# Last unit of an expert layer: its rows reach their tokens by products with one-hot matrices, in place of scatters and reloads

## The chip, the cores and the metric

The kernel runs on one core of one Trainium2 chip. The metric is the device time of one execution in microseconds (us), the median over runs. The core has five engines that work side by side, each in the order of its own instructions: TensorE (PE), VectorE (DVE), ScalarE (ACT), GpSimd (POOL) and SyncE (SP), which here only issues DMAs. POOL also issues the indirect DMAs (gathers and scatters).

## The reference, cut to what matters

The input is x, 16 batches of 1024 tokens of 256 floats. The output is x + attention(xn) + experts(xn), with xn the layer norm of x. The part around the change is the expert layer:

```python
scores = jnp.einsum('ntd,de->nte', x, gate_w)
probs = jnp.transpose(jax.nn.softmax(scores, axis=-1), (0, 2, 1))
g, m = jax.lax.top_k(probs, k)                  # k = 256 tokens for each batch and expert
xin = jax.vmap(lambda xb, mb: xb[mb])(x, m)
h = jax.nn.gelu(jnp.einsum('nekd,edf->nekf', xin, w1))
h = jnp.einsum('nekf,efd->nekd', h, w2)
weighted = g[..., None] * h
out = jnp.zeros((n * t, d)).at[flat_idx].add(weighted.reshape(-1, d))
return out.reshape(n, t, d).astype(jnp.bfloat16)
```

Each of 8 experts picks its 256 tokens of highest probability in each batch, runs them through two layers (256 to 1024, gelu, 1024 to 256), weighs the rows by their probability and adds them to the tokens that they came from. The sum over experts is rounded to bfloat16 and then added to x and attention.

## The kernel before

**Stages.** The attention comes first (some 560 us). It leaves in DRAM, for every batch, `xg` (the normalized rows and gate values), `xa` (x plus attention) and `acc` (zeros, in which the experts' rows are summed). The indices of the chosen tokens lie in `idxT`, on the partitions of the rows that they belong to.

**Units.** The rest is a loop over 64 units. A unit is one expert with one pair of batches: 512 rows, in four quarters q of 128 (q = 2t + k: half t is one batch, k its first or second 128 rows). The batches come in three groups (4, 6 and 6), and inside a group the experts follow one another, each over all pairs. The last three units are expert 7 with the batches 10 and 11, 12 and 13, 14 and 15; instructions of the last two bear 12 and 14 in their tiles' names.

**Order.** The order of every engine's work is written out by hand: what the Python code calls first is issued first. While unit n computes, the rows of unit n+2 are gathered and those of n+1 laid out. `layer1` (L767) has two rounds r = 0, 1, each with three PSUM banks pa, pb, pc of which each gets two products. In each round DVE computes `u2` from pb (L792), later `u3` from pb (L801) and `c22` from pc (L803). PE can begin the second product in pb only when L792 has read it, and the second in pc (after both rounds) only when L803 has. `layer2` (L840) makes the rows y1 (half 1) and y0 (half 0): L899, L903, L904, L905 and L917 on DVE, `fourth_sum` (L836) on POOL, and `weigh` (L867), the multiplication with the probability, on ACT.

**Scatters.** `scatter(y, t, k)` (L871, the DMA at L873) adds the 128 rows of a quarter to their tokens in `acc` of the batch, as an indirect DMA of POOL. The two scatters of a batch write the same tensor, so the second has a wait for the first one's landing. y1's scatters are issued in `layer2`; y0's in `rest`, which runs in the next unit's `layer1`, after the first products of its round 0.

**Finish.** The output is made in 64 parts, four for each batch: a part is two of the eight tokens that each partition holds, 128x512 floats or 256 KB, and token number = 8 x partition + j. A part loads `xa` (`load_x`) and `acc` (`load_a`), adds the bias (`bias`, L994, DVE), rounds acc to bfloat16 (`cast`, L990, ACT), adds (`add`, L999, DVE) and stores (`store`, L1003, SP). `plan` hangs these steps into slots of the units: "first" (ahead of a unit's layer 1), "s1", "s2" (round 0), "s3" (round 1), "middle" (after layer 1), "lay" (in layer 2, where other units lay out the next), "s4" (late in layer 2), and "end" (after the last unit). Lists: `first`, eight parts of batches 11 and 10, done in the last unit; `second` (in the loop `nearly`), batches 13 and 12, reloaded in the last unit's "middle", with their adds after the last unit; `third` (in the loop `last`), batches 15 and 14, reloaded (L986) when the last unit's own scatters have landed.

The tail of `run`, after the last unit:

```python
pending.pop()(lambda: None)          # rest of the last unit: the scatters
for k, p in enumerate(nearly):
    ...
for step in at.pop((NU, "end")):     # five biases
    step()
done.load_last_a()
for p in last:
    done.cast(p)
    done.add(p)
    done.store([p])
```

Of the kernel before, what the change touches and what calls it, by code (L numbers as in the profile page):

```python
# [8 lines left out]
F32 = mybir.dt.float32  # L9
BF16 = mybir.dt.bfloat16  # L10
U32 = mybir.dt.uint32
AF = mybir.ActivationFunctionType
ALU = mybir.AluOpType
AX = mybir.AxisListType

P = 128
# [7 lines left out]
def tile_linear_attn_expert_choice_moe(  # L24
# [648 lines left out]
    with ExitStack() as fctx:  # L673
# [163 lines left out]
                u.half_sum(0, r), u.block(1, 0, r), u.half_sum(1, r), ALU.subtract  # L837
            )

        def layer2(u, rows, w2_sb, wt, lay_out_next, slot, more_sums):  # L840
            (b11, _), (b21, b22) = out_weights(w2_sb)
            t1, t2, t3, t4 = (wt[:, i, :, :] for i in range(4))

            def hidden(i, t):
                return u.hT[:, i * ND : (i + 1) * ND, t * HT : (t + 1) * HT]

            def product(bk, a, b, start=True):
                for k in range(NS):
                    for c in range(ND):
                        nc.tensor.matmul(  # L850
                            bk[:, k * EH : (k + 1) * EH], a[:, c, k * P : (k + 1) * P],
                            b[:, c, :], start=start and k == 0 and c == 0, stop=True,
                            skip_group_check=True,
                        )

            def two(bk):
                return bk[:, 0:E].rearrange("p (k d) -> p k d", k=NS)

            def new(k):
                return bank(f"q{k}{u.e}_{u.b0}")  # L860

            def temp(tag):
                return u.temp(tag, "y")[:, 0, :].rearrange("p (k d) -> p k d", k=NS)

            def weigh(y, t, k, cols, in_):
                q = t * NS + k
                nc.scalar.activation(  # L867
                    y[:, k, cols], in_, AF.Copy, scale=rows[:, q, E + u.e : E + u.e + 1]
                )

            def scatter(y, t, k):  # L871
                b, ix = index(u.e, u.b0, t * NS + k)
                nc.gpsimd.indirect_dma_start(  # L873
                    out=acc[b], out_offset=bass.IndirectOffsetOnAxis(ap=ix, axis=0),
                    in_=y[:, k, :], in_offset=None, compute_op=ALU.add,
                )

            y0, y1 = (
                hpool.tile([P, NS, E], F32, tag="y", name=f"y{t}{u.e}_{u.b0}", bufs=4)
                for t in range(2)  # L880
            )
            px, pw = new("x"), new("w")
            product(px, hidden(0, 0), b11)
            p1 = temp("p1")
            nc.scalar.copy(p1, two(px))
            first_sum(u, 1)
            product(pw, hidden(1, 1), t4)
            for r in range(2):
                second_sum(u, r)
            pz = new("z")  # L890
            product(pz, u.sums[:, 0, :, :], t1)
            for r in range(2):
                third_sum(u, r)
                fourth_sum(u, r)
            lay_out_next()
            py = new("y")
            product(py, u.sums[:, 1, :, :], t2)
            u2 = temp("u2")
            nc.vector.tensor_tensor(u2, two(py), p1, ALU.add)  # L899
            pv = new("v")  # L900
            product(pv, hidden(0, 1), t3)
            u3 = temp("u3")
            nc.vector.tensor_tensor(u3, two(pv), u2, ALU.add)  # L903
            nc.vector.tensor_tensor(y1[:, :, EH:E], two(pz), u3, ALU.add)  # L904
            nc.vector.tensor_tensor(y1[:, :, 0:EH], two(pw), u3, ALU.add)  # L905
            for k in range(NS):
                weigh(y1, 1, k, slice(0, E), y1[:, k, :])
            scatter(y1, 1, 0)
            if more_sums:
                more_sums()  # L910
                scatter(y1, 1, 1)
            product(px, hidden(1, 0), b21, False)
            for k in range(NS):
                weigh(y0, 0, k, slice(0, EH), px[:, k * EH : (k + 1) * EH])
            slot("s4")
            product(pz, u.sums[:, 0, :, :], b22, False)
            nc.vector.tensor_tensor(y0[:, :, EH:E], two(pz), u2, ALU.add)  # L917

            def rest(between):
                for k in range(NS):  # L920
                    weigh(y0, 0, k, slice(EH, E), y0[:, k, EH:E])
                scatter(y0, 0, 0)
                if not more_sums:
                    scatter(y1, 1, 1)
                between()
                scatter(y0, 0, 1)

            return rest


# [4 lines left out]
        class Finish:  # L935
            def __init__(self):
                self.todo = [
                    (b, slice(j, j + 2))
                    for h, e, b0 in units if e == NE - 1
                    for b in (b0 + 1, b0) for j in range(0, NJ, 2)  # L940
                ]
                self.x, self.a, self.s = {}, {}, {}

            def part(self, t, p):
                b, j = self.todo[p]
# [52 lines left out]
            def add(self, p):  # L998
                nc.vector.tensor_tensor(self.x[p], self.x[p], self.s[p], ALU.add)  # L999

            def store(self, ps):
                for p in ps:
                    nc.sync.dma_start(self.part(out, p), self.x[p])  # L1003

        def plan():

            done, at = Finish(), {}

            def put(n, place, step, *args):
                at.setdefault((n, place), []).append(lambda: step(*args))  # L1010

            of = [[p for p, (b, _) in enumerate(done.todo) if b in g] for g in GROUPS]
            ends = [max(n for n, u in enumerate(units) if u[0] == h) + 2 for h in range(3)]

            for k, p in enumerate(of[0] + of[1]):
                n, place = ends[0] + k, "s2"
                if k >= len(of[0]):
                    k -= len(of[0])
                    n = ends[1] + k
                    if n > NU - 7:  # L1020
                        n, place = n - (NU - 6) + ends[1] + 2, "s4"
                put(n - 1, "first", done.load_x, p)
                put(n - 1, "first", done.load_a, p)
                put(n - 1, "s4", done.cast, p)
                put(n, place, done.bias, p)
                put(n, place, done.add, p)
                put(n, place, done.store, [p])

            first, second, third = (of[2][i * 2 * QT : (i + 1) * 2 * QT] for i in range(3))
            assert len(of[2]) == 6 * QT  # L1030
            for k, p in enumerate(first):
                put(NU - 6, "first", done.load_x, p)
                put(NU - 5 + k // 4, "s2" if k % 4 < 2 else "s4", done.bias, p)
                put(NU - 2, "middle", done.load_a, p)
                put(NU - 1, ("s1", "s2", "s3", "lay")[k // 2], done.cast, p)
            put(NU - 3, "first", done.load_last_x)
            for p in second:
                put(NU - 1, "middle", done.load_a, p)
            places = [(NU - 3, "s4")] * 3 + [
                (NU - 2, place) for place in ("s1", "s1", "s2", "s2", "s3", "s4", "s4")  # L1040
            ] + [(NU - 1, "s1")] + [(NU, "end")] * 5
            for p, (n, place) in zip(second + third, places):
                put(n, place, done.bias, p)
            for k, p in enumerate(first):
                place = "s2" if k < 2 else "s3" if k < 4 else "lay"
                put(NU - 1, place, done.add, p)
                put(NU - 1, place, done.store, [p])
            return at, done, second, third

        def run(gen, first):  # L1050
# [19 lines left out]
            def add_sums(n):  # L1070
                for _ in range(n):
                    if sums:
                        sums.pop(0)()
# [10 lines left out]
            for n, (h, e, b0) in enumerate(units):  # L1084
# [14 lines left out]
                def between():  # L1099
                    add_sums(2)  # L1100
                    if n + 2 < NU:
                        rows[n + 2] = gather(*units[n + 2])
# [17 lines left out]
                def lay_out_next():  # L1120
# [4 lines left out]
                    else:  # L1125
# [3 lines left out]
                pending.append(  # L1129
                    layer2(  # L1130
                        u, rows[n], w2s[i], wts[i], lay_out_next, slot,
                        None if final else lambda: add_sums(2),
                    )
                )
                del rows[n]
# [3 lines left out]
            for k, p in enumerate(nearly):  # L1139
                if k >= QT:  # L1140
                    done.cast(p)
                done.add(p)
                done.store([p])
            for step in at.pop((NU, "end")):
                step()
            done.load_last_a()
            for p in last:
                done.cast(p)
                done.add(p)
                done.store([p])  # L1150
            assert not at
# [46 lines left out]
```

## Time and profile before

| what | value |
|---|---|
| median of 3 runs | 2180.11 us (2178.78 to 2180.33) |
| the profiled execution | 2178.58 us |
| its span | 2176.9 us |
| PE busy | 2125.7 us (98%) |
| DVE busy | 1757.8 us (81%) |
| POOL busy | 1357.8 us (62%) |
| ACT busy | 861.9 us (40%) |
| granted clock of TensorE over the span | 0.993 |
| last product of PE ends | 2151.2 us |
| last add of DVE ends | 2172.1 us |

All times count from the start of the span. Lines of the profile name the engine, the line of the kernel, the operation and its tiles as out<-in. "Idle before" is the time for which the engine stood still just ahead of an instruction, with what ended the wait as far as semaphores show it; where the engine that is named had long been done, it was something else, often a DMA. A product of float32 shows up as two passes of PE, so 16 passes are 8 products. SPq stands for the DMA queue of SP.

### The profile page before, as it was taken

Reading aid. Unit: us, or ns where it says so; the run is one execution under the profiler, and the core shown is the slowest. Engines: PE = TensorE matmul, PEld = TensorE weight load, DVE = VectorE, ACT = ScalarE, POOL = GpSimd, SP = SyncE. Lnnn points to the kernel's source line nnn. Section 1 sums busy time; section 2 is a strip of 40 time slices with the busy share of each in tenths; the row PEclk is TensorE's granted clock in tenths of the full one; section 3 lists DMA queues with packets and bytes.
Section 4 is the critical chain, followed back from the end, with each engine's and each line's share of the span. In section 5 each row is a group of like instructions: output and inputs, shape, how many; then the busy total and the mean of one; then the engine's idle time right before and its main releaser. Section 6 shows DMA issues by size and latency. Waiting matters only on the chain.

```text
span 2176.9 us, 37218 instructions
## 1 busy us (share of the span) xinstructions
PE 2125.7 (98%) x13556; PEld 1957.1 (90%) x13556; DVE 1757.8 (81%) x3197; ACT 861.9 (40%) x1598; POOL 1357.8 (62%) x1015
## 2 busy tenths in 40 slices
PE   7999999999999999999999999999999999999995
PEld 6888888888899999999999999899999999999994
DVE  6888888886889989679999998767777788776786
ACT  5645546453233333333333333333334343333334
POOL 4545445354577777777666766676676677667743
PEclk9999999999999999999999999999999999999997
DMA  6444535555455555554555555355546665565567
GB/s 200 137 150 142 194 122 171 164 157 172 113 104 107 104 105 112 111 134 94 132 135 112 129 133 132 69 102 103 116 103 159 168 151 124 131 138 106 118 169 213
DMA packets 333767, 290.61 MB, mean 133 GB/s; under 512 B 163856, under 2 KB 285968, under 8 KB 333584
## 3 DMA queue, kind: packets, MB, share of 16 engines
q1 hardware_dynamic: 283168, 217.55, 35.3%
q0 software_dynamic: 49728, 70.29, 18.2%
q8 instruction: 107, 1.75, 0.3%
q14 instruction: 76, 0.62, 0.1%
q10 hardware_dynamic: 688, 0.40, 0.1%
HBM read 153.36 MB, written 101.19 MB: 117 GB/s over the span
## 4 chain that ended last, share of the span: by engine, by line
PE 93%; DVE 3%; issue 1%; DMA 1%; SPq 1%; ACT 1%; POOL 0%; DVEq 0%; ACTq 0%; POOLq 0%
PE pb L771 14%; PE qz L850 10%; PE qx L850 10%; PE pc L771 10%; PE pa L771 9%; PE pk L318 5%; PE qw L850 5%; PE qv L850 5%; PE qy L850 5%; PE pq L387 5%; PE pg L423 5%; PE po L491 5%; PE xt L305 1%; PE qt L469 1%; SPq L685 1%
## 5 line engine op out<-in xcount | busy, mean ns | idle before, releaser
L873 POOL DMA_INDIRECT acc<-y,idxT x256 | 414.7, 1620 | 350.9 <-ACT y L867 201.1
L237 POOL DMA_INDIRECT rows<-xg,idxT x256 | 263.5, 1029 | 79.4 <-issue 70.5
L867 ACT ACTIVATE y<-y,rows 128x256 f32<-128x256 f32 (+1 forms) x256 | 102.6, 450 | 518.1 <-DVE y L905 516.0
L746 ACT ACTIVATE hT<-hT 128x512 f32<-128x512 f32 x384 | 238.3, 632 | 155.2 <-DVE hT L803 94.6
L771 PE MATMUL pb<-ts,ws 128*128 128x256 f32 x1024 | 263.5, 380 | 4.6 <-DVE ts L721 2.4
L771 PE MATMUL pa<-xT,w 128*128 128x256 f32 x1024 | 263.8, 380 | 1.4 <-issue 1.4
L850 PE MATMUL qx<-w,hT 128*128 128x128 f32 x2048 | 249.4, 275 | 0.0
L850 PEld LDWEIGHTS qx<-w,hT 128*128 128x128 f32 x2048 | 243.9, 192 | 3.3
L836 POOL TENSOR_TENSOR sums<-hT,sums 128x512 f32<-128x512 f32 x128 | 172.7, 1367 | 85.5 <-PE qz L850 84.9
L771 PEld LDWEIGHTS pb<-ts,ws 128*128 128x128 f32 x1024 | 194.1, 190 | 32.6 <-POOL ws L713 2.7
L771 PEld LDWEIGHTS pa<-xT,w 128*128 128x128 f32 x1024 | 190.3, 191 | 25.2 <-issue 1.8
L801 DVE TENSOR_TENSOR u<-pb,p 128x512 f32<-128x512 f32 x128 | 88.4, 691 | 113.2 <-PE pb L771 98.3
L746 ACT ACTIVATE hT<-pa 128x512 f32<-128x512 f32 x128 | 76.5, 597 | 170.0 <-PE pa L771 166.0
L785 ACT COPY p<-pa 128x512 f32<-128x512 f32 x128 | 75.1, 586 | 165.9 <-PE pa L771 161.8
L792 DVE TENSOR_TENSOR u<-pb,p 128x512 f32<-128x512 f32 x128 | 88.5, 691 | 64.0 <-ACT y L867 44.5
L771 PE MATMUL pc<-xT,ws 128*128 128x256 f32 x512 | 134.6, 385 | 0.0
L771 PE MATMUL pc<-ts,ws 128*128 128x256 f32 x512 | 132.3, 381 | 0.0
L771 PE MATMUL pb<-ts,w 128*128 128x256 f32 x512 | 131.4, 379 | 0.0
L850 PE MATMUL qw<-wt,hT 128*128 128x128 f32 x1024 | 124.8, 275 | 0.0
L850 PE MATMUL qz<-wt,sums 128*128 128x128 f32 x1024 | 124.8, 275 | 0.0
L850 PE MATMUL qy<-wt,sums 128*128 128x128 f32 x1024 | 124.8, 275 | 0.0
L850 PE MATMUL qz<-w,sums 128*128 128x128 f32 x1024 | 124.8, 275 | 0.0
(142 smaller groups left out, 4753.1 us busy)
## 6 DMA issues: line engine op xcount, KB each, us to landing
rq<-rows SPq DMA_DIRECT2D x1024, 32.0 KB
w<-in_w_dram SPq DMA_DIRECT2D x96, 256.0 KB
w<-in_w_dram SPq DMA_DIRECT2D x48, 512.0 KB
xg<-xn SPq DMA_DIRECT2D x16, 1056.0 KB
x<-in_x_dram SPq DMA_DIRECT2D x32, 512.0 KB
acc<-zero SPq DMA_DIRECT2D x16, 1024.0 KB
xr<-in_x_dram SPq DMA_DIRECT2D x32, 512.0 KB
xa<-xr SPq DMA_DIRECT2D x28, 512.0 KB
```

The lines of the kernel that those rows point to most:

```text
L237: nc.gpsimd.indirect_dma_start(out=rows[:, q, :], out_offset=None, in_=xg[b], in_offset=bass.IndirectOffsetOnAxis(ap=ix, axis=0),)
L318: nc.tensor.matmul(pk[:, 0:KG], t.xnT[:, d, j * P : (j + 1) * P], wkg_sb[:, d, :], start=(d == 0), stop=(d == NC - 1),)
L387: nc.tensor.matmul(pq[:, k * E : (k + 1) * E], t.xnT[:, d, j * P : (j + 1) * P], wq_sb[:, d, :], start=(d == 0), stop=(d == NC - 1),)
L423: nc.tensor.matmul(t.pg[:, c * E : (c + 1) * E], t.xn[:, j, c * P : (c + 1) * P], t.kk[:, j, 0:E], start=(j == 0), stop=(j == NJ - 1),)
L491: nc.tensor.matmul(po[:, k * E : (k + 1) * E], qT[:, c, j * P : (j + 1) * P], t.mo[:, c, :], start=(c == 0), stop=(c == NC - 1),)
L746: nc.scalar.activation(out, in_, AF.Gelu_apprx_tanh)
L771: nc.tensor.matmul(bk[:, j * HT : (j + 1) * HT], w[:, f * P : (f + 1) * P], x, start=start and j == 0, stop=True, skip_group_check=True,)
L792: nc.vector.tensor_tensor(u2, both(pb), p1, ALU.add)
L836: nc.gpsimd.tensor_tensor(u.half_sum(0, r), u.block(1, 0, r), u.half_sum(1, r), ALU.subtract)
L850: nc.tensor.matmul(bk[:, k * EH : (k + 1) * EH], a[:, c, k * P : (k + 1) * P], b[:, c, :], start=start and k == 0 and c == 0, stop=True, s ...
L867: nc.scalar.activation(y[:, k, cols], in_, AF.Copy, scale=rows[:, q, E + u.e : E + u.e + 1])
L873: nc.gpsimd.indirect_dma_start(out=acc[b], out_offset=bass.IndirectOffsetOnAxis(ap=ix, axis=0), in_=y[:, k, :], in_offset=None, compute_op ...
```

## The change

The last unit (batches 15 and 14) no longer scatters. For each of its four quarters a matrix `hot` is built that has, for slot s (partition) and token, a one where the token is that slot's and zero elsewhere: 1024 columns in float32, in eight blocks (one for each j) of 128. POOL fills the tile with token numbers (`iota`, L1009), DVE copies the quarter's indices to a float column (L1019) and compares the tile with it in place (`is_equal`, L1021). The tiles are old ones: `cur` for quarter 0, `wq_sb` and `wo_sb` (512 columns each) for quarter 1, two buffers of the gathered `rows` for quarters 2 and 3.

A part of batch 15 or 14 is then made by `spread`: for each of its two j, two products of 128x128 by 128x256 (k = 0, 1; the hot block with y) summed in PSUM, so 4 a part and 32 in all, after the unit's last product on PE. DVE adds the part of acc without the last unit's rows, which is now reloaded ahead of the unit (`load_last_a` in slot "first"), and rounds to bfloat16 in the same instruction (L1048). `add` and `store` are as before.

Beside that some steps move: the adds and stores of three of the eight `second` parts, and two of the five biases, go from the end into slot "s4" of the last unit, where DVE does them between L905 and L917.

```diff
-        def layer2(u, rows, w2_sb, wt, lay_out_next, slot, more_sums):
+        def layer2(u, rows, w2_sb, wt, lay_out_next, slot, more_sums, final):
...
-            scatter(y1, 1, 0)
-            if more_sums:
+            if not final:
+                scatter(y1, 1, 0)
                 more_sums()
                 scatter(y1, 1, 1)
...
-                scatter(y0, 0, 0)
-                if not more_sums:
-                    scatter(y1, 1, 1)
-                between()
-                scatter(y0, 0, 1)
+                if not final:
+                    scatter(y0, 0, 0)
+                    between()
+                    scatter(y0, 0, 1)
+
+            u.y = (y0, y1)
...
+            def new_hot(self, q, tiles):
+                n = NJ // len(tiles)
+                parts = [t.rearrange("p (j t) -> p j t", t=P) for t in tiles]
+                for i, t in enumerate(parts):
+                    nc.gpsimd.iota(
+                        t, pattern=[[1, n], [NJ, P]], base=i * n, channel_multiplier=0,
+                        allow_small_or_imprecise_dtypes=True,
+                    )
+                self.hot[q] = [t[:, j, :] for t in parts for j in range(n)]
+                self.hot_parts[q] = parts
+
+            def fill_hot(self, q):
+                h, e, b0 = units[-1]
+                _, ix = index(e, b0, q)
+                nc.vector.tensor_copy(self.slots[:, q : q + 1], ix)
+                for t in self.hot_parts[q]:
+                    nc.vector.tensor_scalar(
+                        t, t, self.slots[:, q : q + 1], None, ALU.is_equal
+                    )
+
+            def new_hots_first(self):
+                self.slots = kpool.tile([P, NQ], F32, tag="slots", name="slots")
+                cur = kpool.tile([P, HALF + 2 * K], F32, tag="cur", name="hot0")
+                self.new_hot(0, [cur])
+                self.new_hot(
+                    1, [t.rearrange("p c e -> p (c e)") for t in (wq_sb, wo_sb)]
+                )
+
+            def new_hots_rest(self):
+                for q in range(2, NQ):
+                    t = gpool.tile([P, NQ, XR], F32, tag="rows", name=f"hot{q}")
+                    self.new_hot(q, [t.rearrange("p q d -> p (q d)")[:, 0 : NJ * P]])
+
+            def spread(self, p, y, t):
+                _, js = self.todo[p]
+                pr = bank(f"pr{p}")
+                for i, j in enumerate(range(js.start, js.stop)):
+                    for k in range(NS):
+                        nc.tensor.matmul(
+                            pr[:, i * E : (i + 1) * E], self.hot[t * NS + k][j], y[:, k, :],
+                            start=(k == 0), stop=(k == NS - 1),
+                        )
+                self.s[p] = hpool.tile([P, 2, E], BF16, tag="fb", name=f"fb{p}", bufs=5)
+                nc.vector.tensor_tensor(
+                    self.s[p], pr.rearrange("p (j d) -> p j d", j=2), self.a[p], ALU.add
+                )
...
             put(NU - 3, "first", done.load_last_x)
+            put(NU - 1, "first", done.load_last_a)
+            put(NU - 1, "first", done.new_hots_first)
+            for q, place in enumerate(("s1", "s2", "s3", "lay")):
+                put(NU - 1, place, done.fill_hot, q)
+            put(NU - 1, "s2", done.new_hots_rest)
             for p in second:
                 put(NU - 1, "middle", done.load_a, p)
+            for p in second[0:3]:
+                put(NU - 1, "s4", done.add, p)
+                put(NU - 1, "s4", done.store, [p])
...
-            ] + [(NU - 1, "s1")] + [(NU, "end")] * 5
+            ] + [(NU - 1, "s1")] + [(NU - 1, "s4")] * 2 + [(NU, "end")] * 3
...
-                        None if final else lambda: add_sums(2),
+                        lambda: add_sums(2), final,
...
-                done.add(p)
-                done.store([p])
+                if k >= 3:
+                    done.add(p)
+                    done.store([p])
             for step in at.pop((NU, "end")):
                 step()
-            done.load_last_a()
-            for p in last:
-                done.cast(p)
+            for k, p in enumerate(last):
+                done.spread(p, u.y[1 - k // QT], 1 - k // QT)
                 done.add(p)
                 done.store([p])
```

More of the change, by code (lines that the diff above doesn't have):

```diff
@@ L942, in __init__ @@
                 self.x, self.a, self.s = {}, {}, {}
+                self.hot, self.hot_parts = {}, {}
             def part(self, t, p):
```

## The prediction

> **What bounds the kernel now.** I read the page first. PE is busy 98% of the span at a granted clock of 0.99, so nearly anything that stops PE costs its full length, and what follows PE's last product is pure addition. The chain of waits (the work that ended last, in order of time: start, length, what) gives that end:
>
> ```profile
> 2149.42 1.80 PE qz L850 x16
> 2151.25 0.44 DVE y L917
> ...
> 2152.38 8.08 DMA acc<-y,idxT x2
> ...
> 2160.85 5.88 DMA fa_rq<-acc
> ...
> 2169.46 2.67 DVE fx_ws L999 x4
> ```
>
> PE ends at 2151.2; then two scatters in a row (8.1 us), the reload of acc (5.9), casts and adds. The last add ends at 2169.46 + 2.67 = 2172.13; the span, 2176.9, ends 4.8 later, when the last store has landed. So 25.7 us stand behind PE, and these the change attacks.
>
> The change also puts new work on POOL and DVE beside the last unit's layer 1. So next I read the timeline there, engine by engine (start, length, engine, line, operation, [idle before it <- what ended it]). POOL, which has the scatters of the unit before the last (rows one to four) and its own step of the last unit (row five):
>
> ```profile
> 2125.31 1.80 POOL L873 DMA_INDIRECT acc<-y,idxT  x1 [3.42 <-ACT y L867]
> 2130.15 1.58 POOL L873 DMA_INDIRECT acc<-y,idxT  x1 [3.03 <-ACT y L867]
> 2132.03 1.54 POOL L873 DMA_INDIRECT acc<-y,idxT  x1 [0.30 <-ACT fb L990]
> 2136.64 1.54 POOL L873 DMA_INDIRECT acc<-y,idxT  x1 [3.07 <-ACT fb L990]
> 2143.86 3.69 POOL L836 TENSOR_TENSOR sums<-hT,sums 128x512 f32<-128x512 f32 x2 [5.67 <-PE qz L850]
> ```
>
> In program order these are y1/0, y1/1, y0/0, y0/1. The two of one batch add into the same acc: the second stands idle 3.0 us and starts 4.84 and 4.61 after the first, though the ACT instruction named had long ended. So POOL is blocked until the first has landed. DVE in the same stretch, which layer 1 needs:
>
> ```profile
> 2128.41 0.69 DVE L792 TENSOR_TENSOR u<-pb,p 128x512 f32<-128x512 f32 x1 [0.78 <-PE pb L771]
> 2130.93 0.69 DVE L801 TENSOR_TENSOR u<-pb,p 128x512 f32<-128x512 f32 x1 [0.63 <-PE pb L771]
> 2132.72 0.69 DVE L792 TENSOR_TENSOR u<-pb,p 128x512 f32<-128x512 f32 x1 [0.31 <-PE pb L771]
> 2135.97 0.69 DVE L803 TENSOR_TENSOR hT<-pc,u 128x512 f32<-128x512 f32 x1
> ```
>
> DVE has only 0.3 to 0.8 us to spare before each. PE writes pb again at 2129.86, 0.76 after the first of these has read it, and pc of round 1 again at 2136.77, 0.1 after the last of them ends at 2136.66. A late DVE stops PE at once.
>
> **Part 1: the matrices, which stand in a queue.** The last unit's "first" slot is issued after y1/0 and y1/1 of the unit before and ahead of y0/0 and y0/1. POOL's order becomes: y1/0, y1/1, iota hot0 (1024 columns), two iotas for hot1 (512 each), y0/0, y0/1, iotas hot2 and hot3 (1024 each), then L836. DVE compares hot0 in slot s1, ahead of the first L792; hot2 in s3, ahead of the second L801 and L803. Both engines work in order, so DVE, and with it PE, waits for POOL, and POOL for scatters to land.
>
> No iota is in the trace. Bounds, with the price of a fill of DVE (a TENSOR_SCALAR whose scalar is a column), come from these groups (busy, mean ns):
>
> ```profile
> L246 POOL MEMSET zero<- 128x512 f32 x1 | 0.5, 522 | 0.0
> L79 POOL TENSOR_SCALAR_AFFINE_SELECT mask<-mask 128x128 f32<-128x128 f32 x1 | 0.3, 347 | 0.0
> L365 POOL TENSOR_TENSOR s<-kk 128x1024 f32<-128x1024 f32 x16 | 37.9, 2371 | 65.4 <-DVE kk L332 65.4
> L332 DVE TENSOR_TENSOR kk<-kk,ke 128x1024 f32<-128x1024 f32 x32 | 39.0, 1219 | 0.0
> L289 DVE TENSOR_SCALAR xn<-x,rstd,nm 128x256 f32<-128x256 f32 x4 | 1.8, 488 | 0.9 <-POOL nm L280 0.9
> ```
>
> Memsets of 128 and 512 columns (0.20, 0.52) give 0.82 ns a column: 0.94 for 1024, the low end. TENSOR_TENSOR gives 2.37 (1.28 for 512), the high end. The affine select also works out a pattern: 0.33 less 0.10 fixed (a memset of one column) over 128 columns is 1.8 ns each, 1.9 for 1024. An iota reads nothing, so I take 1.7 and, for 512, 0.9, nearer to that row than to the memset. A fill: L289 takes 0.41 at least for 256 columns, L125 0.28 for 128: 1.0 ns a column and 0.15 fixed, so 1.2 for 1024 (as L332) and 0.67 for 512; the copies of the indices 0.2 each (L356).
>
> The clock, then:
> - A vector instruction of POOL begins 1.0 after the scatter ahead of it (1977.37 to 1978.45): hot0 2131.15 to 2132.85. DVE fills it until 2134.2; with the bias (0.62) behind it, L792 ends at 2135.5, not 2129.1. PE stands 5.6 us, from 2129.9.
> - hot1 is there at 2134.65 and costs no further wait. y0/0 starts 0.35 later (1981.62 to 1981.97), at 2135.0; y0/1 4.6 after it, at 2139.6; hot2 runs 2140.6 to 2142.3. DVE has by then done all of round 0, the fill of hot1 (1.3) included, by about 2140.5, and waits.
> - Fill until 2143.55, two adds (0.62 each), L801, then L803 0.79 after L801's start, with 0.69 of its own: 2146.3 against 2136.66. PE's pc of round 1 comes **9.6 us later**.
>
> The second stall takes the first one in, so they do not add. After it L836 is no hindrance (hot3's iota ends at 2144.0, L836 is wanted at 2143.86 + 9.6). Hot3's fill (1.4 with its copy) falls into DVE's idle 0.70 before L899 and 1.36 before L903: nothing. The eight reloads of acc are moved to SP ahead of the unit (their tiles are free after the transposes that end at 2119.4): at 0.33 to 0.65 an issue done before y1/0's data move, and the stores queued behind them on SP start only at 2129.7: nothing; if they do slow that scatter, the chain above slips by as much, at most the 1 to 2 us that 2 MB take at the 400 GB/s of the last stretch beyond 2125. With the iota bounds the shift is 7.4 to 11.7.
>
> **Part 2: the tail.** Removed: four scatters, the wait for them, eight reloads, eight casts. Added: 32 products of 128x256 on PE. A pg group (16 passes, 8 such products) takes 3.46, so 0.43 each, 13.8 in all: in before's clock 2151.2 to 2165.1. y1 is weighed by then; y0 (L917, then 0.7 on ACT) by 2153.2, and is used from 2158. Per part of four products (1.73 on PE) DVE adds twice: 0.79 until the dependent one can start, 0.61 until the next, 1.40.
>
> But DVE has other work first. From L905's end (2148.9): three adds and two biases, now in s4, at 0.62 (2152.0); L917 (2152.4); one add; four adds that wait for casts on ACT behind y0's weighing (2156.3); three biases (2158.2). Then 8 x 1.40 = 11.2: **2169.4**. So DVE, not PE, ends the tail; from PE alone it would be 2165.1 + 0.2 + 1.4 = 2166.7. Against 2172.13 this gains 2.7. The stores now come 1.4 apart and not 0.6, so less is queued; of the 4.8 behind the last add I take off 0.2. The tail gains **2.9** (5.6 at best).
>
> **The sum.** +9.6 - 2.9 = +6.7 us. The profiled execution took 2178.58, 1.5 below the median of the runs shown (2180.11): 2185.3 by the one, **2186.8** by the median, which I give. A kernel of this length can be told from no change beyond 0.2%, 4.4 us.
>
> **A rule that speaks against it.** The clock can be seen to fall where PE stops (window, then busy times, PEclk third from the end):
>
> ```profile
> 2153.00:2154.00 1.00, 0.00 (x0) 0.00 (x0) 1.00 (x3) 1.00 (x3) 1.00 (x1) 0.99 0.90 328
> 2154.00:2155.00 1.00, 0.00 (x0) 0.00 (x0) 1.00 (x3) 0.47 (x1) 0.70 (x2) 0.50 1.02 371
> ```
>
> It is halved 2.8 us after PE's last product. A stall of 5.6 would do the same; the products then run at half speed for a while (at the start 32 pk passes took 8.46, later 7.12: 1.3 lost). This loss falls before the second stall, which then is only shorter: nothing in my sum, up to 2.8 if the second stall, 2 to 3.4 long, halves the clock too. [...]
>
> **Rivals.**
> - **The matrices' price is higher**, by iotas slower than any row, or the clock lost in the second stall: each us on 1024 columns costs 3 us of shift (hot0, both halves of hot1, hot2). For: POOL's power on 8 columns takes 1.7 us. Against: no simple form does. +9 to +15: 2189 to 2195.
> - **Cheap matrices, a shorter tail**: iotas at the memset's rate (shift 7.4) and the tail set by PE (5.6): +1.8, 2181.9. For: an iota only writes. Against: DVE's list above.
> - **POOL isn't held**: the iotas run while a scatter is in flight. It decides if hot2 is there by 2135.6, 6.7 sooner than I have it. Then only the fills stay: 3.7 and three copies, 4.3 in layer 1, against 2.35 of DVE's idle: 2.0 late, less 2.9: -0.9, 2179.2; by PE's tail -3.6, 2176.5. For: the releaser named in the rows isn't a scatter. Against: every second scatter of a batch stands the same 3.0 idle.
>
> **Chances.** Forecast (+4.4 to +9) 0.53, higher price 0.22, cheap matrices 0.16, POOL not held 0.09. The last two are mostly within 0.2%; a fifth or so of the cheap case comes out slower after all, a third of the last faster. Faster 0.03, same 0.20, slower 0.77. Range: +1.4 (cheap) to +11.9 (TENSOR_TENSOR's rate, 8.8, and 2.8 of clock): 2181.5 to 2192.
>
> **What would show it.** In the changed profile: the DVE compare of hot0 and of hot2 idle with POOL's iota as releaser; PE idle some 5.6 and 2 to 3.4 us in layer 1 of the last unit; PE's last L850 near 2161; DVE without gaps in the last 11 us while PE is ahead of it. I am wrong if the iotas start before y1/1, or if PE shows no gap.

## The result and the profile after

The changed kernel takes 2182.97 us against 2178.45 us for the kernel before on the same chips (medians of 22 runs each; lowest 2181.91 and 2177.18): ratio **1.0022, 95% interval 1.0016 to 1.0028**, or +4.5 us. The forecast was +6.7, the range +1.4 to +11.9. One of the changed kernel's 22 runs (3764.7 us) and two of e5's below (3776.4 and 5833.8) were in a much slower state and are left out of the ratios. The profiled execution took 2182.9, its span 2181.2.

The last unit's first product (PE's first pa, L771) began at 2126.40 before and 2124.81 after, and between 2124.85 and 2127.32 in the experiments that show no new stall ahead of it: single profiles scatter by up to 2.5 us over the 2100 us that the change does not touch. So stretches are counted from that product.

POOL in the timeline of the changed kernel (start, length, engine, line, operation, [idle before <- what ended it]):

```profile
2123.72 1.80 POOL L873 DMA_INDIRECT acc<-y,idxT  x1 [3.43 <-ACT y L867]
2129.58 1.55 POOL L873 DMA_INDIRECT acc<-y,idxT  x1 [4.05 <-ACT hT L746]
2130.58 1.62 POOL L1009 IOTA hot<- 128x1024 f32 x1
2131.57 1.17 POOL L1009 IOTA wq_sb<- 128x512 f32 x1
2132.09 1.66 POOL L1009 IOTA wo_sb<- 128x512 f32 x1
...
2133.92 1.55 POOL L873 DMA_INDIRECT acc<-y,idxT  x1 [0.17 <-issue]
2138.43 1.54 POOL L873 DMA_INDIRECT acc<-y,idxT  x1 [2.96 <-DMA out_dram<-fx]
2139.42 2.58 POOL L1009 IOTA hot<- 128x1024 f32 x2
```

The order is the predicted one: y1/0, y1/1, the iotas, y0/0, y0/1, the iotas. No iota starts before the second scatter of a batch has been let go, 5.86 and 4.51 after the first. DVE and then PE, in the same view:

```profile
2132.23 1.05 DVE L1021 TENSOR_SCALAR hot<-hot,slots 128x1024 f32<-128x1024 f32 x1 [6.73 <-POOL hot L1009]
...
2133.80 0.68 DVE L792 TENSOR_TENSOR u<-pb,p 128x512 f32<-128x512 f32 x1
...
2141.06 1.49 DVE L1021 TENSOR_SCALAR hot<-hot,slots 128x1024 f32<-128x1024 f32 x1 [0.90 <-POOL hot L1009]
...
2151.35 0.75 DVE L1021 TENSOR_SCALAR hot<-hot,slots 128x1024 f32<-128x1024 f32 x1
```

```profile
2134.53 2.08 PE L771 MATMUL pb<-ts,ws 128*128 128x256 f32 x4 [6.10 <-DVE slots L1019]
...
2145.13 1.13 PE L771 MATMUL pc<-xT,ws 128*128 128x256 f32 x4 [1.51 <-DVE hT L803]
```

The first two of these compares (hot0, hot2) wait for an iota, the third (hot3) does not; PE stands twice, 6.1 and 1.5 us, where 5.6 and 2 to 3.4 were forecast. (The releaser named for the first, L1019, is the copy for hot1, which starts at 2134.40, just as L792 ends; what PE needs is L792, which stands behind the compare of hot0 and a bias.) The first wait also halves the clock (a window and its busy times, PEclk third from the end):

```profile
2131.50:2131.75 0.25, 0.00 (x0) 0.00 (x0) 0.00 (x0) 0.00 (x0) 0.25 (x2) 0.71 0.50 29
...
2138.25:2138.50 0.25, 0.25 (x3) 0.21 (x2) 0.00 (x0) 0.09 (x1) 0.07 (x1) 0.63 1.04 393
```

0.71 in a quarter of a microsecond puts the fall at 2131.6, 3.2 after PE's last product ended (2128.44); 0.63 puts the return at 2138.4, 3.9 after PE went on. The tail, in the chain of waits:

```profile
2165.42 1.81 DVE fx_ws L995 x3
2167.23 0.61 DVE fb L1048
...
2176.43 0.70 DVE fb L1048
2177.15 0.69 DVE fx_ws L1000
```

Scatters, their landing and the reloads are gone; the chain is DVE's list alone, biases and then sixteen adds, until 2177.84.

All runs can be read from one table, of one profile each. It splits the stretch from the last unit's first product to the end of the span at three events: PE's pc of round 1, which waits for L803 (PE's L771 `pc<-xT,ws` of that round), the end of L905, and the end of the last add (us).

| kernel | to pc, round 1 | to L905's end | L905's end to last add | last add to end | whole |
|---|---|---|---|---|---|
| before | 10.37 | 22.48 | 23.25 | 4.77 | 50.5 |
| after | 20.32 | 33.50 | 19.53 | 3.36 | 56.4 |
| e1, first iotas earlier | 17.80 | 32.44 | 19.52 | 3.34 | 55.3 |
| e5, e1 with PE kept busy | 18.00 | 31.18 | 19.53 | 3.36 | 54.1 |
| e4, reloads later | 19.29 | 32.49 | 19.52 | 3.32 | 55.3 |
| e8, iotas one scatter up | 13.16 | 26.35 | 19.52 | 3.31 | 49.2 |
| e2, all iotas far ahead | 10.57 | 23.83 | 19.53 | 3.36 | 46.7 |
| e3, e2 with fills early | 10.37 | 22.48 | 19.53 | 3.36 | 45.4 |
| e6, e2 with fills placed | 10.36 | 22.48 | 19.59 | 3.31 | 45.4 |
| e7, e6 with biases on POOL | 10.37 | 22.48 | 21.21 | 3.34 | 47.0 |
| e9, more products | 20.00 | 33.20 | 19.54 | 3.37 | 56.1 |
| e10, more adds | 19.92 | 33.10 | 21.72 | 3.33 | 58.2 |

The change pushes L905 back by 11.0 us (by 10.7 and 10.6 in e9 and e10, whose edits come behind it) and shortens what follows it from 28.0 to 22.9, by 5.1: +5.9 in the profiles, +4.5 in the medians. The intervals of most experiments' medians overlap those of their neighbours, so differences of a microsecond between them are read from these stretches.

### The profile page after: what moved, and what is told of

Same layout as the page of the kernel before. It is cut to its first block, busy times and chain, and to the rows that moved or that the text cites. A ratio compares the mean times of both kernels' runs of the same rounds, so it can differ in the third digit from the quotient of the medians.

```text
span 2181.2 us, 37370 instructions
## 1 busy us (share of the span) xinstructions
PE 2141.3 (98%) x13620; PEld 1970.0 (90%) x13620; DVE 1764.8 (81%) x3214; ACT 855.9 (39%) x1590; POOL 1353.9 (62%) x1016
## 5 line engine op out<-in xcount | busy, mean ns | idle before, releaser
L873 POOL DMA_INDIRECT acc<-y,idxT x252 | 406.0, 1611 | 343.0 <-ACT y L867 188.3
L771 PE MATMUL pb<-ts,ws 128*128 128x256 f32 x1024 | 265.5, 382 | 10.8 <-DVE slots L1019 6.1
L771 PE MATMUL pa<-xT,w 128*128 128x256 f32 x1024 | 263.9, 380 | 1.4 <-issue 1.4
L771 PEld LDWEIGHTS pb<-ts,ws 128*128 128x128 f32 x1024 | 195.3, 191 | 39.4 <-DVE slots L1019 6.5
L836 POOL TENSOR_TENSOR sums<-hT,sums 128x512 f32<-128x512 f32 x128 | 172.5, 1369 | 93.6 <-PE qz L850 93.6
L771 PEld LDWEIGHTS pa<-xT,w 128*128 128x128 f32 x1024 | 190.4, 191 | 25.2 <-issue 1.8
L792 DVE TENSOR_TENSOR u<-pb,p 128x512 f32<-128x512 f32 x128 | 88.4, 691 | 64.0 <-ACT y L867 44.3
L771 PE MATMUL pc<-xT,ws 128*128 128x256 f32 x512 | 134.7, 385 | 1.5 <-DVE hT L803 1.5
L771 PE MATMUL pc<-ts,ws 128*128 128x256 f32 x512 | 132.1, 381 | 0.0
L771 PE MATMUL pb<-ts,w 128*128 128x256 f32 x512 | 131.4, 379 | 0.0
```

What stands on the lines that cost most here:

```text
L771: nc.tensor.matmul(bk[:, j * HT : (j + 1) * HT], w[:, f * P : (f + 1) * P], x, start=start and j == 0, stop=True, skip_group_check=True,)
L792: nc.vector.tensor_tensor(u2, both(pb), p1, ALU.add)
L836: nc.gpsimd.tensor_tensor(u.half_sum(0, r), u.block(1, 0, r), u.half_sum(1, r), ALU.subtract)
L873: nc.gpsimd.indirect_dma_start(out=acc[b], out_offset=bass.IndirectOffsetOnAxis(ap=ix, axis=0), in_=y[:, k, :], in_offset=None, compute_op ...
```

## The experiments

Theory: POOL's queue, held by the second scatter of each batch, delays the iotas, and with them DVE and PE; the tail gains. Rivals: the matrices' own price (iotas and fills) is what costs; the clock is; the tail's gain is set by PE.

### e1: the first two matrices' iotas earlier

"gap" is a new slot between the two scatters of y1 of a unit; NU - 3 is the third unit from the end.

```diff
-                        lambda: add_sums(2), final,
+                        lambda: (add_sums(2), slot("gap")), final,
-            put(NU - 1, "first", done.new_hots_first)
+            put(NU - 3, "gap", done.new_hots_first)
```

> The changed kernel, with the three iotas of hot0 and hot1 issued one unit and a half earlier, between the two scatters of y1 of the unit with batches 10 and 11; hot2 and hot3 stay behind y0/1. Changed minus before was +4.5 us. Theory (the second wait decides and takes in the first): the 6.1 us stall of PE goes, y0/0 follows y1/1 by 1.9 instead of 4.3 us, so hot2 comes 2.4 sooner and the kernel is some 2.4 faster than the changed one: +2.1 over before, with one stall of PE of 4 to 6 us left. Rival (the two stalls add): 6.1 us faster than the changed one, -1.6. Rival (DVE's fills cost, not the waits): no change, +4.5.

Measured: 2182.50 against 2178.28, ratio 1.0017 (1.0008 to 1.0026), +4.2. The first stall is gone, but PE in the timeline of e1 shows:

```profile
2143.60 2.07 PE L771 MATMUL pc<-xT,ws 128*128 128x256 f32 x4 [7.28 <-DVE hT L803]
2145.47 1.91 PE L771 MATMUL pb<-ts,w 128*128 128x256 f32 x4
```

pc comes 2.5 sooner, as it should when POOL is freed of three iotas, yet only 1.1 of it is left at L905. The two stalls have become a single one of 7.3, and behind that the products run at half speed (2.07 and 1.91, against 1.13 and 1.03 after). In the changed kernel the halved clock fell into a stretch that ended in a second wait, which swallowed it; here nothing does. The forecast of +2.1 missed this: right for the queue, without the clock.

### e5: e1, with PE kept busy in the stall

Sixteen products that nobody reads (32 passes) are added ahead of that pc; this is work beyond the reference's.

```diff
...
+                    if r and final:
+                        for _ in range(8):
+                            product(pa, 1, a11, b11, True)
                     product(pc, r, s4, b22, False)
...
```

> The kernel with the first three iotas early, plus 16 products of 128x256 on PE (6.9 us at the full clock) whose result nobody reads, placed where PE stands 7.3 us in the last unit, ahead of pc of round 1. Theory (the stall ends when POOL and DVE are ready, and halves the clock, which then costs 1.7 us: from there to qx it took 3.6 us, 1.8 at the full clock): PE is ready all the same, the clock stays, and the kernel is 1.7 us faster with more work, some +2.5 over before, and the two products after the stall take 1.0 each, not 2.07 and 1.91. Rival (those products are slow for another reason, or DVE paces them): no gain, +4.2. Rival (the added products reach past the stall): slower.

Measured: 2181.76 against 2179.05, ratio 1.0013 (1.0003 to 1.0022), +2.7. PE in the timeline of e5:

```profile
2137.39 7.07 PE L771 MATMUL pa<-xT,w 128*128 128x256 f32 x32
2145.03 1.13 PE L771 MATMUL pc<-xT,ws 128*128 128x256 f32 x4 [0.57 <-DVE hT L803]
```

More work took less time in this stretch: pc no sooner (18.00 against 17.80), but from it to L905's end 13.2 instead of 14.6. So 1.5 us is the price of the clock here, with the queue unchanged: in the products behind the stall the granted clock is 0.50 in e1 (1.00 until 2140.0, 0.50 from 2146.0 to 2147.0, back at 2147.3) and 1.00 in e5.

### e2: all iotas far ahead

The iotas of all four matrices go into "gap" of the fourth unit from the end; hot2 then takes the tiles `wv_sb` and `wkg_sb`, hot3 two `probs` tiles, all idle by then. The fills stay.

```diff
-            put(NU - 1, "first", done.new_hots_first)
-            put(NU - 1, "s2", done.new_hots_rest)
+            put(NU - 4, "gap", done.new_hots_first)
+            put(NU - 4, "gap", done.new_hots_rest)
...
```

> The changed kernel, with all iotas issued three units earlier, between the scatters of y1 of the unit with batches 14 and 15 of expert 6, where POOL stands idle; hot2 and hot3 lie in tiles of their own (the weights of the attention and the probabilities, no longer read). The fills stay where they are. Theory (the waits behind scatters are the loss): both stalls go, what stays are the fills, 3 us and 0.6 for the copies against 2.35 us of idle time, 1 to 1.5 late, less the 5.1 us that the tail gained: -3.5 to -4.2 over before. Rival (the fills and moved adds on DVE are the loss): at or above +2. Rival (the tail gained only the 2.9 of the prediction): -1.5 to -2.

Measured: 2174.33 against 2178.28, ratio 0.9983 (0.9974 to 0.9992), **-3.9**. With the same columns to make and to fill (hot2 and hot3 now in two halves each), at another place in POOL's queue, the change becomes a gain: neither the matrices' price nor the products cost the time, the wait does. What is left is nearly all in slot "lay" (pc comes 0.2 later than before, L905 1.35). DVE in the timeline of e2:

```profile
2143.41 4.65 DVE L1000 TENSOR_TENSOR fx<-fx,fb 128x512 f32<-128x512 f32 x4
```

The same four adds take 2.49 in e6, where hot3's fill isn't ahead of them: they start 1.2 before POOL's L836 there (2142.61, 2143.77), and 0.2 before it here (2143.41, 2143.59).

### e3: the fills early too

```diff
-            for q, place in enumerate(("s1", "s2", "s3", "lay")):
-                put(NU - 1, place, done.fill_hot, q)
+            for q, place in enumerate(("s1", "s2", "s3", "s3")):
+                put(NU - 3, place, done.fill_hot, q)
```

> As the kernel with all iotas early, and the four fills in the unit with batches 10 and 11 of expert 7 (slots s1, s2, s3, s3), where DVE idles 1.4 to 1.8 us ahead of the instructions that follow. Theory: nothing is left in the last unit's layer 1, so the whole gain of the tail shows: -5 over before, 1 to 1.5 faster than with the fills in the last unit. Rival (the fills were hidden anyway): the same as with the iotas alone early. Rival (two fills in one slot exceed 1.83 us of idle time there): no better than it either, but with a gap on PE in that earlier unit.

Measured: 2175.09 against 2178.28, ratio 0.9984 (0.9975 to 0.9993), -3.2, where -5 was expected. The last unit does not show the loss: its stretch is 45.4, as short as e6's. It is in the earlier unit, which DVE's timeline of e3 shows:

```profile
2078.96 2.62 DVE L1021 TENSOR_SCALAR hot<-hot,slots 128x1024 f32<-128x1024 f32 x1 [1.23 <-POOL hot L1009]
```

A fill of 1024 columns takes 0.75 with POOL idle (hot3's in the changed kernel). This one waited for the iota, and then ran beside the other six, for 2.62; PE stood 1.57 there. The same wait, in another place.

### e6: each fill where DVE has room

```diff
+            for q, (n, place) in enumerate(
+                ((NU - 3, "s2"), (NU - 3, "s3"), (NU - 2, "s3"), (NU - 1, "s1"))
+            ):
+                put(n, place, done.fill_hot, q)
...
```

With e2's iotas; the bias that stood in s1 of the last unit goes to POOL in "lay".

> All iotas early as before, and each fill in a slot with idle time on DVE and no iota running: hot0 and hot1 in s2 and s3 of the unit with batches 10 and 11, hot2 in s3 of the next unit, hot3 in s1 of the last, whose bias goes to POOL. Theory (with neither waits nor fills in the way, the whole gain of the tail shows, 5.1 us by the stretch from the last unit's first product to the end of the span in the kernel with early fills, 45.4 against 50.5 us): -5 over before and no gap on PE in the three last units. Rival (the fills cost wherever they stand): -3.5 to -4.

Measured: **2173.71 against 2179.05, ratio 0.9978 (0.9969 to 0.9987), -5.3**: the best version, faster than both kernels. PE's rows show no idle time in the last three units. L905 comes at 22.48, where it came before, and the whole gain of the tail, 5.1, is kept. DVE in the timeline of e6:

```profile
2142.61 2.49 DVE L1000 TENSOR_TENSOR fx<-fx,fb 128x512 f32<-128x512 f32 x4
...
2148.72 1.88 DVE L1000 TENSOR_TENSOR fx_wt<-fx_wt,fb 128x512 f32<-128x512 f32 x3
```

### e7: e6, with the five last biases on POOL too

```diff
...
-                    put(n, place, done.bias, p)
+                    put(NU - 1, "lay", done.bias, p, nc.gpsimd)
...
```

> As the kernel with placed fills, and the five late biases, two ahead of L917 and three ahead of the parts, on POOL behind L836 of the last unit. Theory (DVE, not PE, sets the end of the tail, by 1.9 us in the kernel with early fills: last add 42.0 us after the unit's first product, 40.1 by PE's last product): 1.5 to 1.9 faster than with placed fills, -6.5 to -7 over before, and the last parts wait for PE. Rival (PE sets the end): no change against placed fills. Rival (POOL's adds and DVE's shut each other out): slower than placed fills.

Measured: 2175.40 against 2179.05, ratio 0.9984 (0.9975 to 0.9993), -3.7: worse than e6, as its rival had it. DVE in the timeline of e7, where POOL adds its biases from 2146.37 to 2155.58:

```profile
2147.67 5.09 DVE L1000 TENSOR_TENSOR fx_wt<-fx_wt,fb 128x512 f32<-128x512 f32 x3
```

Three adds take 5.09 and not 1.88 beside POOL's adds, so DVE lost 3.2 in these three alone, more than the five biases (0.6 each) would have cost it. The tail got 1.6 longer.

### e8: the iotas one scatter further up

```diff
-            put(NU - 1, "first", done.new_hots_first)
-            put(NU - 1, "s2", done.new_hots_rest)
+            put(NU - 2, "gap", done.new_hots_first)
+            put(NU - 1, "between", done.new_hots_rest)
...
```

"between" is a new slot between y0/0 and y0/1. Each group of iotas moves past a single scatter.

> The changed kernel, same tiles, same slots for the fills, with the iotas moved by one scatter: those of hot0 and hot1 between y1/0 and y1/1 of the unit before the last, those of hot2 and hot3 between y0/0 and y0/1, so that POOL makes them while it would wait for a landing. Theory (only the place behind a waiting scatter is the fault): hot0 is there at 1.0 + 1.6 us after y1/0, 1.3 too late for L792; hot2 costs 1 to 1.5 at L803; the rest is the tail's gain: -2.5 to -3.5 over before. Rival (the scatters, pushed back by the iotas, come to bear on the reloads and casts of the tail): around 0 or above.

Measured: 2178.29 against 2179.05, ratio 0.9995 (0.9987 to 1.0004), -0.8. POOL in the timeline of e8:

```profile
2126.23 1.80 POOL L873 DMA_INDIRECT acc<-y,idxT  x1 [3.42 <-ACT y L867]
2127.50 1.59 POOL L1009 IOTA hot<- 128x1024 f32 x1
...
2131.93 1.55 POOL L873 DMA_INDIRECT acc<-y,idxT  x1 [1.29 <-ACT hT L746]
```

The iotas run right behind the first scatter (hot0's starts 1.27 after it), in what was POOL's idle time; the second starts 5.70 after the first, about as in the changed kernel (5.86). So a scatter in flight does not hold the iotas; what holds them in the changed kernel is the second scatter, which waits at the head of the queue (POOL idle for 4.05 ahead of it there). 7.2 of the 9.95 us at pc go away. The expectation of -2.5 to -3.5 was too good: PE still stands 0.48 and 1.89, since the compares of hot0 and hot2 still wait for their iotas (1.12 and 0.81) and then run beside the next ones (1.05 and 1.49), and "lay" costs its 1.1 as in e2 (from pc to L905's end 13.2; before 12.1).

### e4: the reloads of acc back behind layer 1

```diff
-            put(NU - 1, "first", done.load_last_a)
                 put(NU - 1, "middle", done.load_a, p)
+            put(NU - 1, "middle", done.load_last_a)
```

> The changed kernel, with the eight reloads of acc moved from ahead of the last unit to behind its layer 1. Theory (the reloads slow the scatter y1/0, whose landing holds the queue of POOL; the second starts 5.86 us after the first, 4.84 without them): the gap is 4.8 again and the kernel 1.0 faster than the changed one, +3.5 over before. Rival (the longer gap has another cause): +4.5 and the same gap. Rival (SP's queue then holds the stores of the tail): slower than +4.5.

Measured: 2183.05 against 2178.28, ratio 1.0022 (1.0013 to 1.0031), +4.8. POOL in the timeline of e4:

```profile
2124.88 1.80 POOL L873 DMA_INDIRECT acc<-y,idxT  x1 [3.43 <-ACT y L867]
2129.64 1.55 POOL L873 DMA_INDIRECT acc<-y,idxT  x1 [2.95 <-ACT y L867]
```

The distance of y1/1 from y1/0 is 4.76, against 5.86 after and 4.84 before, and PE's first stall 5.0 and not 6.1; the stretch is 1.1 shorter (to pc, 0.6 to 1.0 against the changed kernel, e9 and e10, which are the same up to there). The median shows none of it. Of the ten profiles with early reloads, nine have a distance of 5.1 to 5.9; but e6 has 4.67 with the same reloads. So the reloads mostly lengthen the first scatter's landing; that they cost the time a microsecond is likely, and not settled.

### e9 and e10: which engine ends the tail

In e9, PE makes the four products of the first part twice; in e10, DVE makes L1048 of the first three parts twice. The same values are written again.

```diff
-                for i, j in enumerate(range(js.start, js.stop)):
+                again = 2 if p == len(self.todo) - 2 * QT else 1
+                for i, j in [*enumerate(range(js.start, js.stop))] * again:
```

```diff
+                for _ in range(2 if p < len(self.todo) - 2 * QT + 3 else 1):
                     nc.vector.tensor_tensor(
```

> The changed kernel, with the four products of the first of the eight parts made twice (the same values, written twice): 1.73 us more for TensorE in the tail, nothing more for VectorE. Theory (VectorE ends the tail): TensorE's last product ends 1.7 later in the stretch from the last L850, still ahead of VectorE's reading of it (before this edit it lay 2.46 ahead: 2173.97 against 2176.43), VectorE's rows stay without gaps and the time stays that of the changed kernel, 2183.0, within 0.5. Rival (TensorE ends the tail): 1.7 more, 2184.7, and VectorE's L1048 waits for TensorE.

> The changed kernel, with VectorE's L1048 of the first three of the eight parts made twice (the same values, written twice): 3 x 0.61 = 1.8 us more for VectorE in the tail, nothing more for TensorE. Theory (VectorE ends the tail): 1.8 more than the changed kernel, 2184.8, and the stretch from the end of L905 to the end of the span grows from 22.9 to 24.7. Rival (TensorE or the stores end the tail): no change, 2183.0, and a stretch of 22.9 to 23.2.

Measured, both against 2178.94: e9 2183.35, ratio 1.0020 (1.0011 to 1.0029), the same as the changed kernel; e10 2185.40, ratio 1.0031 (1.0020 to 1.0043). In the table, from L905's end to the last add, e9 has 19.54 and e10 21.72, against 19.53: 1.73 us more on PE cost nothing, three adds on DVE (0.72 each) cost 2.2. (Their intervals overlap; the stretches tell them apart.) In e9, where L1043 and L1048 are one line further down, PE and DVE in the timeline:

```profile
2176.08 0.59 PE L1044 MATMUL pr<-y,wo_sb 128*128 128x256 f32 x2
```

```profile
2177.42 0.68 DVE L1049 TENSOR_TENSOR fb<-pr,fa_ts 128x512 bf16<-128x512 f32 x1
```

Even so PE's last product ends (2176.67) 0.75 ahead of its reader. DVE ends the tail.

## Why the prediction was right, and where its terms were off

**The wait, +9.6: right.** pc of round 1 comes 9.95 later. The mechanism is shown by e2, e6 and e8: iotas out of that place in the queue, no wait. Its parts were off in both directions:
- *The iota, 1.7.* The compare starts 1.65 after its iota starts, so as a wait the price was right. But POOL starts the next one after 0.99 (1024 columns) or 0.52 (512), the memset's rate, the low bound. The three of hot0 and hot1 held the queue for 3.3 in all, to y0/0's start (1.83 after the third one's), where 3.85 had been reckoned.
- *The fill, 1.2.* It takes 0.75 alone (e2: 0.76; 0.49 for 512), and 1.05 and 1.49 in the changed kernel, beside an iota. The row of 256 columns that it was taken from did not scale, and the 1.22 of L332 is no measure for it: from 512 to 1024 columns the fill grows by 0.26 (0.49 to 0.75), a tensor_tensor by 0.53 (0.69 of L1000 to 1.22 of L332).
- *The reloads, nothing.* y1/1 came 1.0 later after y1/0 than before, and with late reloads (e4) it did not. The prediction's own second figure, 1 to 2 us, was the better one: the cover that it named, the early issue, most likely did not hold.

That these nearly cancel is luck: counted from the last unit's first product as before has it (+1.59), hot2's compare starts at 2142.65 where 2142.3 was forecast.

**The second stall takes in the first and its clock: right.** e1 is the counter-proof, 1.5 us lost where no second stall follows, and e5 gives them back. Four profiles have both stalls (e4, after, e10, e9): there the clock came back 3.0, 3.9, 4.5 and 5.7 after PE went on, the second stall was 2.04, 1.51, 1.23 and 0.64, and pc came at 19.3, 20.3, 19.9 and 20.0. The later the clock, the shorter the second stall, and pc does not follow it. Neither the fall nor the return has one delay here: the fall came 2.8 (before) and 3.2 (after) after PE's last product, and 5.4 at the end of the changed kernel (0.79 in the quarter from 2179.25, PE's last product having ended at 2173.97); the return came 3.0 to 5.7 after PE went on.

**Hot3's fill in "lay", nothing: wrong.** It fits the idle time by itself, but pushes four adds on to POOL's L836, where they take 4.65 and not 2.49. Lost: 0.89 (the fill and its copy) + 2.16 - 2.06 (DVE's idle time) = 1.0; from pc to L905 the table has 1.1, and e6, without it, none.

**The tail, -2.9: the right engine, too small a gain, -5.1.** DVE ends it (e9, e10). The loop runs at 1.33 a part, not 1.40 (10.7 and not 11.2 in all: 0.5), the list ahead of it is 0.5 shorter, and from the last add to the end it takes 3.36, not 4.6 (1.2). The last is the largest: the last stores now come 1.33 apart, before 0.6 to 0.7. That this spacing is the cause is only argued: every run with the new tail has 3.3 to 3.4, but none varies it. Nor does a run move the adds and biases into "s4" alone; that they would have gained nothing by themselves is argued from before's rows, where DVE waits 5.2 and 2.1 us in the tail for reloaded parts of acc.

**The sum.** +9.95 + 1.1 - 5.1 = +5.9, by its own profile, where +6.7 was forecast; a cost left out (1.1) and a gain undersized (2.2) partly cancelled, so that the total came so close is in part luck. The rest to the +4.5 of the medians is within what two profiles differ by ahead of the last unit.

The ends of the range are a little wider than the terms named for them: 7.4 - 5.6 is +1.8 and not +1.4, 8.8 + 2.8 is +11.6 and not +11.9. No run shows the 2.8 of clock: behind the second stalls, 0.64 to 2.04 long, the products run at full speed (1.13 and 1.03, e4, after, e10, e9), and the loss that was measured is 1.5 (e1).

**The rivals.** Higher price: no, the price was lower, and the second stall, 1.5 long, did not halve the clock (1.00 from 2145 on). Cheap matrices with a shorter tail: its tail (5.1 of 5.6) came true, its iotas in part. POOL goes on at the memset's rate, but what waits for an iota waits 1.65 and more. That costs 1.0 ahead of y0/0 (3.3 where 0.94 + 0.52 + 0.52 + 0.35 had been reckoned) and 0.7 at hot2's compare (1.65 and not 0.94); with 1.0 by the longer landing, the shift of 7.4 comes to 10.1, about the 9.95 measured. POOL isn't held: false of the changed kernel's order; but e8 shows how near it lay.

## What to carry to other kernels

An instruction that costs a microsecond costs what stands ahead of it in its engine's queue: look for the last instruction there that waits for a transfer, and put independent work in front of it, far ahead if its tile is free. Then place what depends on it by the room of the engine that executes it, and look at which engine it pushes its neighbours on to. When two stalls follow one another, removing one may only lengthen the other, with the clock's loss laid bare.

## What the runs showed of the hardware that was not expected

- Iotas on POOL overlap: each is shown as 1.6 us for 1024 columns, yet the next starts 0.99 after it (0.52 for 512).
- DVE takes longer beside POOL's work: a compare of 0.75 takes up to 2.62 beside iotas (e3), three adds 5.09 and not 1.88 beside POOL's adds (e7). What sets these sizes is shown by no run.
- Products that nobody reads gained time: e5 against e1, 1.2 us of stretch. PE's mean granted clock from 2131 to 2147 was 1.00 in e5.
- The halved clock's loss depends on what follows: 1.5 us in e1, nothing measurable in the four profiles in which a second wait ends the stretch.
